# Re-pricing transfers in a kernel's own plan: side by side, with a later landing

## The chip, the core and the metric

The kernel runs on one core of one Trainium2 chip. The metric is the device time of one execution in microseconds. The core has five engines, each with an instruction queue that it works off in order: TensorE (PE: matmuls and transposes), VectorE (DVE), ScalarE (ACT), GpSimd (POOL) and SyncE (SP, which here does nothing but issue transfers). An instruction whose inputs are not there holds up everything behind it in its own queue.

## What is computed

Two layers over x of shape (32, 512, 128), that is 32 images of 512 nodes with 128 features, with one adjacency matrix of 512 x 512 shared by all. Cut to what matters:

```python
h = relu(layernorm(x))                                     # layer 0
x = x + leaky_relu(softmax_attention(h @ W, adj), 0.3)     # graph attention
h = relu(layernorm(x))                                     # layer 1
for _ in range(5):                                         # gated recurrence
    m = adj @ h                                            # for every image
    z = sigmoid(m @ w3a.T + m @ w3b.T + h @ u3.T + ...)
    r = sigmoid(m @ w4a.T + m @ w4b.T + h @ u3.T + ...)
    hv = tanh(m @ w5a.T + m @ w5b.T + (r * h) @ u5.T + ...)
    h = (1 - z) * h + z * hv
x = x + h
```

The five steps of an image depend on each other; the 32 images don't.

## The kernel before

An image goes through `layer0` once and then through `recurrence` five times. The state of an image is held turned (`hT`: features on the partitions) for the gates, and as rows (nodes on the partitions, split into a high and a low fp16 half, `hi` and `lo`) for the product with the adjacency. One step on PE is: m from `hi` and `lo` (8 matmuls, L1031), g for the reset gate (L1050, L1051), v for the candidate (L1089, L1090) and g again for the update gate (L1071). ACT takes the results out of PSUM (L1042, L1056, L1078, L1095), and DVE makes the products and the new state (L1063, L1101, L1107, L1110).

At the end of a step the new state must be turned into rows. For the first three images and near the end PE does that (`turn`, L1124). In all other steps it goes through DRAM: DVE transposes blocks of 32 x 32 (`blocks`, L1137), SP stores them (`way`, L1143), and after the store four loads fetch a quarter of the rows each (`rows`, L1148). ACT then makes `hi` (L1008) and DVE makes `lo` (L1006), and PE can start the next step. The loads wait for the store alone, and write separate partitions of the same tile.

`layer0` does the same kind of thing on POOL's queue from the fifth image on. `blockwise` turns an image in four stores and one load, once for the attention's input (`turn_a`, L733, and the load into `h0T`, L746) and once for the recurrence's (`turn_b`, and the load into `hT`). The attention's destination scores go out in four small stores (`line`, L866) and come back spread over all partitions (`es`, L879).

None of this is issued in the order of the loops. Every piece of work is a `Task` with an engine, a modelled duration, a key (its due time), the tasks that it needs and the buffers that it uses. `plan` simulates the engines: again and again it takes, among the tasks that can begin earliest, the one with the lowest key, and notes when its result is seen. The tasks are then issued in that order, and the order within each engine's queue is what the chip runs. Three things of the model concern this change:

```python
COST = {... "POOL": (650, 0, 130), "SP": (430, 0, 0)}    # ns per task: fixed, per column, until seen
seen = begin + t.ns + t.lands                            # lands: LANDING for a transfer
f.last = max(f.last, seen)                               # a buffer is free again when its last use is seen
```

A transfer takes 430 ns on SP or 650 ns on POOL to issue, and its result is seen `LANDING` ns later (1500 ns more for the big loads of `blockwise` and for `es`). A task can begin only when all that it needs is seen. Buffers are counted by tag (`BUFFERS`): there are two of `blocks` (shared by the turns of layer 0 and of the recurrence), three of `rows`, four each of `way`, `turn` and `line`, and two of `res`, the results on their way out. The plan's needs are for the order only: the waits of the program itself follow from what each instruction reads and writes.

Of the kernel before, what the change touches and what calls it, by code (L numbers as in the profile page):

```python
# [44 lines left out]
    "SP": (430, 0, 0),  # L45
}
FIRST_IDLE, IDLE = 32, 36
LANDING = 2600
BRANCH = 150

WAIT = {"DVE": 200, "ACT": 200}
# [232 lines left out]
def gat_then_gated_gnn_kernel(  # L284
# [40 lines left out]
    def add(*args, **kwargs):  # L325
        tasks.append(Task(*args, **kwargs))
        return tasks[-1]
# [127 lines left out]
    t = add("PE", [1024], soon, issue, (a_dst_loaded,), (f_as,), at=4300)  # L455
# [56 lines left out]
    t = add("POOL", [1] * 3, 0, issue, (rest_loaded,))  # L512
# [9 lines left out]
    t = add("PE", [256] * 5, 0, issue, (t,), (f_ws, f_us))  # L522
# [55 lines left out]
    t = add("DVE", [1] * 4, late, issue, (*counted, wa_made))  # L578
# [7 lines left out]
    t = add("PE", [256], late, issue, (t,), (f_viol,))  # L586
# [130 lines left out]
    def blockwise(dst, src, which, keys, needs, buffers, by_halves):  # L717


        f, way = Buffer("blocks"), Buffer("turn")  # L720

        def blocks():
            pin(nc.vector.transpose(
                new(f, f"blocks_{which}"), src().rearrange("p k d -> p (k d)")
            ))

        t = add("DVE", [512], keys(0), blocks, needs, (*buffers, f))

        def store(g):
            def issue():  # L730
                if way.tile is None:
                    new(way, f"turn_{which}", (K * P, P))
                pin(nc.gpsimd.dma_start(  # L733
                    out=way.tile.rearrange("(e r) (g q) -> g r e q", r=Q, g=G)[g],
                    in_=f.tile[ts(g, Q)].rearrange("r (e q) -> r e q", q=Q),
                ))

            return issue

        stores = []  # L740
        for g in range(G):
            stores.append(add("POOL", [1], keys(1), store(g), (t, *stores[-1:]), (f, way),
                              lands=LANDING))

        def load():
            pin(nc.gpsimd.dma_start(  # L746
                out=dst().rearrange("p (k m) -> p k m", k=K),
                in_=way.tile.rearrange("(k p) m -> p k m", k=K),
            ))

        return add("POOL", [1], keys(2), load, stores, (*buffers, way), lands=LANDING + 1500)

# [10 lines left out]
    def layer0(b):  # L763
# [7 lines left out]
        def keys(i):  # L771
            return begin + length * (base[0] + i) / parts
# [10 lines left out]
        t = relu_layernorm(h, lambda: f_x.tile, f"a{b}", keys, (loaded,), (f_x, f_h), b == 0)  # L783
        base[0] = 5
        turn = transposed if direct else blockwise
        t = turn(hT, h, f"a{b}", keys, t, (f_h, f_hT), b == 0)
# [5 lines left out]
        def hw():  # L792
            return f_hw.tile or new(f_hw, f"hw_{b}", (P, K, D + 3))
# [40 lines left out]
        if direct:  # L834
            f_es = Buffer("g", "bank")

            def spread(half):
                def issue():
                    es = f_es.tile or new(f_es, f"es_{b}")
                    for k in range(2 * half, 2 * half + 2):  # L840
                        pin(nc.tensor.transpose(
                            es[:, ts(k, P)], hw()[:, k, D + 1 : D + 2].to_broadcast([P, P]), ident
                        ))

                return issue

            t = None
            for half in range(2):
                t = add("PE", [256] * 2, keys(0), spread(half), (made[half], t), (f_hw, f_es))
        else:  # L850
            f_es, f_lines, way = Buffer("es"), Buffer("lines"), Buffer("line")
            rep = Q // K

            def gather():
                pin(nc.vector.transpose(
                    new(f_lines, f"lines_{b}", (P, Q)).rearrange("p (k e) -> p k e", k=K),
                    hw()[:, :, D + 1 : D + 2].to_broadcast([P, K, rep]),
                ))

            t = add("DVE", [64], keys(0), gather, made, (f_hw, f_lines))  # L860

            def store(k):
                def issue():
                    if way.tile is None:
                        new(way, f"line_{b}", (K, P))
                    pin(nc.gpsimd.dma_start(  # L866
                        out=way.tile[k].rearrange("(g q) -> g q", g=G),
                        in_=f_lines.tile[k * rep :: Q],
                    ))

                return issue

            stores = []
            for k in range(K):
                stores.append(add("POOL", [1], keys(1), store(k), (t, *stores[-1:]),
                                  (f_lines, way), lands=LANDING))

            def spread():
                pin(nc.gpsimd.dma_start(  # L879
                    out=new(f_es, f"es_{b}"),  # L880
                    in_=way.tile.rearrange("k p -> (k p)").partition_broadcast(P),
                ))

            t = add("POOL", [1], keys(2), spread, stores, (way, f_es), lands=LANDING + 1500)
        base[0] = 15
# [92 lines left out]
        if by_halves:  # L978
            joined = []
            for part, ks in enumerate((slice(0, K // 2), slice(K // 2, K))):  # L980
                t = add("DVE", [256], keys(0.3 * part), lambda ks=ks: leak(ks), averaged[part : part + 1],
                        (f_o,))
                joined.append(add("DVE", [256], keys(0.3 * part), lambda ks=ks: join(ks), (t,),
                                  (f_o, f_x)))
        else:
            t = add("DVE", [512], keys(0), lambda: leak(slice(0, K)), averaged, (f_o,))
# [8 lines left out]
        t = relu_layernorm(hN, lambda: x1, f"b{b}", keys, joined, (f_hN,), False)  # L995
        base[0] = 26
        halved = halves(b, hN, keys(0), t, (f_hN,))
        t = turn(lambda: hTs[b % SLOTS], hN, f"b{b}", keys, t, (f_hN,), False)
# [13 lines left out]
    def recurrence(b, step, halved, turned):  # L1012
# [5 lines left out]
        def keys(i):  # L1018
            return key + i * STEP / 4
# [19 lines left out]
        t = add("PE", [493] * K, keys(0), aggregate("hi", True), (high, *adjacency), (f_m,))  # L1039
        t = add("PE", [493] * K, keys(0), aggregate("lo", False), (t, low), (f_m,))  # L1040
# [12 lines left out]
        t = add("PE", [2048] * 2, keys(2), gate_r, (t_m, turned, *weights), (f_g, f_mT))  # L1053
# [21 lines left out]
        t = add("PE", [2048], keys(3), gate_z, (t_r,), (f_g, f_mT))  # L1075
# [16 lines left out]
        t = add("PE", [2048] * 2, keys(3), candidate, (t_rh,), (f_v, f_mT, f_rh))  # L1092
# [4 lines left out]
        t = add("ACT", [512], keys(4), tanh_v, (t,), (f_v, f_hv))  # L1097
# [14 lines left out]
        t = add("DVE", [512], keys(5), differ, (t,), (f_hv, f_d))  # L1112
        t = add("DVE", [512], keys(5), gated, (t, t_z), (f_z, f_d))
# [3 lines left out]
        if nth < 5 * SHORT or (step >= STEPS - 2 and b >= B - SHORT_END):  # L1117

            f = Buffer("o", "bank")

            def turn():
                h_ps = new(f, f"h_{b}_{step}")
                for k in range(K):
                    pin(nc.tensor.transpose(h_ps[:, ts(k, P)], hT[:, ts(k, P)], ident))  # L1124

            needs = (add("PE", [256] * K, keys(6), turn, (turned,), (f,)),)
            view = ("p k d -> p k d", {})

            def src():
                return f.tile.rearrange("p (k d) -> p k d", k=K)  # L1130
        else:


            f_b, way, f = Buffer("blocks"), Buffer("way"), Buffer("rows")

            def blocks():
                pin(nc.vector.transpose(  # L1137
                    new(f_b, f"blocks_{b}_{step}").rearrange("p (g k q) -> p g k q", g=G, k=K),
                    hT.rearrange("p (k g q) -> p g k q", g=G, k=K),
                ))  # L1140

            def store():
                pin(nc.sync.dma_start(out=new(way, f"way_{b}_{step}"), in_=f_b.tile))  # L1143

            def load(g):
                def issue():
                    rows = f.tile or new(f, f"rows_{b}_{step}", (P, G, N // G))
                    pin(nc.sync.dma_start(  # L1148
                        out=rows[ts(g, Q)],
                        in_=way.tile.rearrange("(a q) (g e) -> g q a e", a=G, g=G)[g],  # L1150
                    ))

                return issue

            t = add("DVE", [512], keys(6), blocks, (turned,), (f_b,))
            t = add("SP", [1], keys(6), store, (t,), (f_b, way), lands=LANDING)
            needs = []
            for g in range(G):
                needs.append(add("SP", [1], keys(6), load(g), (t, *needs[-1:]), (way, f),
                                 lands=LANDING))  # L1160
            view = ("p k (a q) -> p a k q", {"a": G})

            def src():
                return f.tile.rearrange("p a (k q) -> p a k q", k=K)
# [18 lines left out]
        if view[1]:  # L1183
            t = add("ACT", [480], keys(8), lower, needs, (f, f_res))
# [147 lines left out]
```

## Time and profile before

| | |
|---|---|
| runs shown | 1143.91, 1145.57, 1149.21 us; median 1145.57 |
| profiled execution | 1144.8 us; its span on the core 1142.7 us |
| granted PE clock | 1.0 |
| busy: PE, DVE, ACT, POOL | 1133.5, 940.6, 659.9, 350.0 us |
| DMA traffic | 132.88 MB, mean 116 GB/s |
| recurrence turns through DRAM | 146 stores, 584 loads |
| turns of layer 0 through DRAM | 28 images, 112 stores each of turn_a, turn_b and line |

Busy times are those of one profiled execution. PE's matmuls overlap in the record (the end of one is modelled and lies past the start of the next), so the rate at which they start says more than their busy time. The profile also gives the chain of waits that ended last, the list of who waited for whom, and for each transfer the time from its issue to its landing.

### The profile page before, as it was taken

The page shows a single profiled execution, that of the slowest core. Times are in us where ns is not written, and L with a number is a line of the kernel's source. Part 1 is how long each engine was busy: PE and PEld are TensorE (multiplying, and loading weights), DVE is VectorE, ACT ScalarE, POOL GpSimd, SP SyncE. Part 2 cuts the span into 40 slices and gives each one's busy share as a digit, 9 for nine tenths or more (in the row PEclk, how much of TensorE's full clock was granted, in tenths as well). Part 3 has the DMA queues.
Part 4 walks back from the last instruction along what each step waited for, and adds up shares of the span by engine and source line. Part 5 has one row for each costly group of instructions (what it writes and reads, how often), then busy time and mean ns, then how long its engine had stood idle before and what let it go on. Part 6 is the DMA issues. An engine that isn't in the chain of part 4 may idle for free.

```text
span 1142.7 us, 15158 instructions
## 1 busy us (share of the span) xinstructions
PE 1133.5 (99%) x4373; PEld 598.5 (52%) x4373; DVE 940.6 (82%) x2124; ACT 659.9 (58%) x1297; POOL 350.0 (31%) x503
## 2 busy tenths in 40 slices
PE   9999999999999999999999999999999999999998
PEld 8665554554555545555554555555555555444444
DVE  7888887887879979889898888799889988667664
ACT  6665656456556465647556646655655655555553
POOL 4345434123244143244413242432544331100000
PEclk9999999999999999999999999999999999999999
DMA  3114444344354444344543443452455343322311
GB/s 107 44 38 122 115 128 133 112 146 118 104 164 116 136 130 136 116 138 119 146 136 115 126 132 120 139 154 89 133 149 144 116 121 117 107 92 79 102 44 67
DMA packets 133916, 132.88 MB, mean 116 GB/s; under 512 B 22083, under 2 KB 97989, under 8 KB 133701
## 3 DMA queue, kind: packets, MB, share of 16 engines
q1 hardware_dynamic: 116066, 94.89, 26.5%
q0 software_dynamic: 17472, 36.79, 13.0%
q8 instruction: 36, 0.59, 0.2%
q14 instruction: 52, 0.42, 0.1%
q10 hardware_dynamic: 290, 0.20, 0.1%
HBM read 70.39 MB, written 61.40 MB: 115 GB/s over the span
## 4 chain that ended last, share of the span: by engine, by line
PE 91%; DVE 5%; DMA 2%; issue 1%; ACT 0%; SPq 0%; DVEq 0%; ACTq 0%
PE m L1031 23%; PE g L1071 11%; PE v L1090 11%; PE g L1050 11%; PE v L1089 11%; PE g L1051 11%; PE av L922 9%; PE hp L806 2%; DMA rows<-way 1%; DVE hT L1110 1%; DVE pt L891 1%; DVE blocks L1137 1%; DVE lo L1006 1%; PE h L1124 1%; DVE d L1101 0%
## 5 line engine op out<-in xcount | busy, mean ns | idle before, releaser
L1056 ACT ACTIVATE rs<-g,zrb 128x512 f32<-128x512 f32 x160 | 109.7, 686 | 143.9 <-PE g L1051 133.4
L1101 DVE SCALAR_TENSOR_TENSOR d<-hv,hT 128x512 f32<-128x512 f32 x159 | 108.4, 682 | 78.3 <-ACT hv L1095 78.0
L1095 ACT ACTIVATE hv<-v,vb 128x512 f32<-128x512 f32 x159 | 108.8, 684 | 104.8 <-PE v L1090 104.2
L1042 ACT COPY mT<-m 128x512 f32<-128x512 f32 x160 | 93.6, 585 | 123.7 <-PE m L1031 121.1
L1031 PE MATMUL m<-adjT,hi 128*128 128x512 f16 x640 | 162.6, 379 | 1.8 <-ACT hi L1008 1.8
L1050 PE MATMUL g<-hT,u3T 128*128 128x512 f32 x320 | 163.5, 593 | 0.0
L1051 PE MATMUL g<-mT,w4sT 128*128 128x512 f32 x320 | 163.5, 592 | 0.0
L1071 PE MATMUL g<-mT,w3dT 128*128 128x512 f32 x320 | 163.1, 593 | 0.0
L1031 PE MATMUL m<-adjT,lo 128*128 128x512 f16 x640 | 162.1, 379 | 0.4 <-DVE lo L1006 0.4
L1089 PE MATMUL v<-mT,w5sT 128*128 128x512 f32 x318 | 162.4, 592 | 0.0
L1090 PE MATMUL v<-rh,u5hT 128*128 128x512 f32 x318 | 162.4, 592 | 0.0
L1078 ACT ACTIVATE zs<-g,zrb 128x512 f32<-128x512 f32 x160 | 109.6, 686 | 59.6 <-PE g L1071 56.6
L1063 DVE SCALAR_TENSOR_TENSOR rh<-rs,hT 128x512 f32<-128x512 f32 x160 | 108.6, 682 | 40.8 <-ACT rs L1056 40.3
L922 PEld LDWEIGHTS av<-hw,pt 128*128 128x128 f32 x1024 | 122.0, 191 | 17.8 <-issue 13.6
L922 PE MATMUL av<-hw,pt 128*128 128x129 f32 x1024 | 123.2, 275 | 0.2 <-ACT adjT L497 0.2
L1110 DVE SCALAR_TENSOR_TENSOR hT<-d,hT 128x512 f32<-128x512 f32 x159 | 109.7, 690 | 11.3
L1031 PEld LDWEIGHTS <-hi 128*128 128x128 f16 x640 | 62.5, 98 | 103.0 <-issue 46.7
L1107 DVE SCALAR_TENSOR_TENSOR d<-zs,d 128x512 f32<-128x512 f32 x159 | 109.6, 689 | 4.5
L1137 DVE STREAM_TRANSPOSE blocks<-hT 128x512 f32<-128x512 f32 x146 | 102.7, 706 | 5.3 <-DMA way<-blocks 3.2
L1031 PEld LDWEIGHTS <-lo 128*128 128x128 f16 x640 | 62.4, 98 | 84.7 <-issue 14.2
L644 POOL TENSOR_TENSOR rs_b<-ve_b,mhalf 128x4 f32<-128x4 f32 x32 | 37.2, 1162 | 224.7 <-DVE ve_b L624 188.4
L1051 PEld LDWEIGHTS g<-mT,w4sT 128*128 128x128 f32 x320 | 60.7, 190 | 76.7 <-issue 71.5
(135 smaller groups left out, 1443.7 us busy)
## 6 DMA issues: line engine op xcount, KB each, us to landing
way<-blocks SPq DMA_DIRECT2D x146, 256.0 KB, 2.1
rows<-way SPq DMA_DIRECT2D x584, 64.0 KB, 2.1
x<-in_x_dram SPq DMA_DIRECT2D x32, 256.0 KB, 2.9
out_dram<-res SPq DMA_DIRECT2D x31, 256.0 KB, 2.1
turn_a<-blocks_a POOLq DMA_DIRECT2D x112, 64.0 KB, 2.3
h0T<-turn_a POOLq DMA_DIRECT2D x28, 256.0 KB, 3.5
es<-line POOLq DMA_DIRECT2D x28, 256.0 KB, 3.8
turn_b<-blocks_b POOLq DMA_DIRECT2D x112, 64.0 KB, 2.3
```

The source lines that it names most:

```text
L922: pin(nc.tensor.matmul(avs()[:, i, :], lhsT=f_pts[c].tile[:, ts(2 * part + i, P)], rhs=hw()[:, c, : D + 1], start=start, stop=(c == K - 1) ...
L1031: pin(nc.tensor.matmul(f_m.tile, lhsT=part[:, k, :], rhs=adjT[:, k, :], start=(first and k == 0), stop=(not first and k == K - 1),))
L1050: pin(nc.tensor.matmul(g, lhsT=u3T, rhs=hT, start=True, stop=False))
L1051: pin(nc.tensor.matmul(g, lhsT=w4sT, rhs=f_mT.tile, start=False, stop=True))
L1056: pin(nc.scalar.activation(new(f_r, f"rs_{b}_{step}"), f_g.tile, AF.Tanh, bias=rb, scale=0.5))
L1071: pin(nc.tensor.matmul(f_g.tile, lhsT=w3dT, rhs=f_mT.tile, start=False, stop=True, skip_group_check=True))
L1078: pin(nc.scalar.activation(new(f_z, f"zs_{b}_{step}"), f_g.tile, AF.Tanh, bias=zb, scale=0.5))
L1089: pin(nc.tensor.matmul(v, lhsT=w5sT, rhs=f_mT.tile, start=True, stop=False))
L1090: pin(nc.tensor.matmul(v, lhsT=u5hT, rhs=f_rh.tile, start=False, stop=True))
L1107: pin(nc.vector.scalar_tensor_tensor(d, f_z.tile, 1.0, d, ALU.add, ALU.mult))
L1110: pin(nc.vector.scalar_tensor_tensor(hT, f_d.tile, 0.5, hT, ALU.mult, ALU.add))
L1137: pin(nc.vector.transpose(new(f_b, f"blocks_{b}_{step}").rearrange("p (g k q) -> p g k q", g=G, k=K), hT.rearrange("p (k g q) -> p g k q", ...
```

## The change

It touches the plan's model alone, in two ways. The constant `LANDING` goes from 2600 to 5000 ns, in every place where it is used: the stores and loads of both kinds of turn, the scores' stores, and the stores of results. And the four stores of a layer-0 turn, the four stores of the scores and the four loads of a recurrence turn no longer need one another: each needs only the task before the group. The program has the same instructions on the same engines; the order in the queues is planned anew.

```diff
-LANDING = 2600
+LANDING = 5000
...
         for g in range(G):
-            stores.append(add("POOL", [1], keys(1), store(g), (t, *stores[-1:]), (f, way),
+            stores.append(add("POOL", [1], keys(1), store(g), (t,), (f, way),
                               lands=LANDING))
...
             for k in range(K):
-                stores.append(add("POOL", [1], keys(1), store(k), (t, *stores[-1:]),
+                stores.append(add("POOL", [1], keys(1), store(k), (t,),
                                   (f_lines, way), lands=LANDING))
...
             for g in range(G):
-                needs.append(add("SP", [1], keys(6), load(g), (t, *needs[-1:]), (way, f),
+                needs.append(add("SP", [1], keys(6), load(g), (t,), (way, f),
                                  lands=LANDING))
```

## The prediction

> **What bounds the kernel now.** I read the shares first, then the chain, then who TensorE (PE) waited for, then the transfers that the change re-prices. The page's first part and its chain:
>
> ```profile
> PE 1133.5 (99%) x4373; PEld 598.5 (52%) x4373; DVE 940.6 (82%) x2124; ACT 659.9 (58%) x1297; POOL 350.0 (31%) x503
> PE 91%; DVE 5%; DMA 2%; issue 1%; ACT 0%; SPq 0%; DVEq 0%; ACTq 0%
> ```
>
> PE is busy in 99% of the span and is 91% of the chain. Busy time alone can hide gaps, as matmuls overlap, so I checked the rate in the chain between 300 and 330 us:
>
> ```profile
> 299.93 3.45 PE m L1031 x16
> 303.38 0.86 PE g L1050 x2
> 304.24 0.86 PE g L1051 x2
> ...
> 327.98 1.78 PE av L922 x16
> ```
>
> A pass of m takes 3.45/16 = 0.216 us, a pass of g or v 0.43, one of av 0.111, and these rates hold all through. The stream's length follows: 1280 m x 0.2156 = 276.0, 1596 g and v x 0.429 = 684.7, 1024 av x 0.1116 = 114.2, 256 hp x 0.112 = 28.7, some 184 transposes and fillers x 0.11 = 20.2, the rest about 5: **1129 us**, the same in any order. The span is 1142.7. Of the 13.7 between, 1.4 come before PE's first matmul, 5.3 after its last, and about 7 are gaps. PE's waits, all of them:
>
> ```profile
> PE m L1031 <- ACT hi L1008: 1.8, 1, 1.8
> PE idle L434 <- POOL ident masks.py:199: 1.4, 1, 1.4
> PE m L1031 <- DVE lo L1006: 0.4, 1, 0.4
> PE h L1124 <- DVE hT L1110: 0.2, 1, 0.2
> PE av L922 <- ACT adjT L497: 0.2, 1, 0.2
> ```
>
> Only the first and third, 2.2 us, lie in the body. The first has its cause in the very transfers at issue (chain, 308 to 323 us):
>
> ```profile
> 315.59 0.43 SPq L1148
> ...
> 316.06 4.55 DMA rows<-way
> ...
> 321.13 0.61 ACT hi L1008
> ...
> 321.79 1.04 PE m L1031 x4
> ```
>
> One rows load took 4.55 us where the plan reckoned 2.6. The transfers as a whole (part 6, last column issue to landing), and the spread for the rows loads alone:
>
> ```profile
> way<-blocks SPq DMA_DIRECT2D x146, 256.0 KB, 2.1
> rows<-way SPq DMA_DIRECT2D x584, 64.0 KB, 2.1
> turn_a<-blocks_a POOLq DMA_DIRECT2D x112, 64.0 KB, 2.3
> h0T<-turn_a POOLq DMA_DIRECT2D x28, 256.0 KB, 3.5
> es<-line POOLq DMA_DIRECT2D x28, 256.0 KB, 3.8
> DMA to landing us min/median/max: 1.7/2.1/4.9
> ```
>
> So 2.6 is a fair figure for the median, 5.0 one for the worst landing.
>
> **What the skill says.** The Trainium skill, "Perfetto Trace Analysis", Identifying the Most-Contended Engine, warns that matmul busy share is a bad measure of headroom; hence the rate above. "TensorE: Matmul & The Clock Gate", Back-to-back issue gap, gives about N/2.4 + 2.5 ns for a warm isolated matmul, 216 ns at N = 512; the trace's 216 agrees, so PE has no slack inside its stream (the lower sustained figure of 131 that the section also gives is not seen here). "DMA: Bandwidth & Descriptors", Anatomy of one DMA, puts a fixed 2.0 us on a transfer, mostly the receipt of the write; the 2.1 for 64 KB and for 256 KB alike agree. Transfers side by side share that cost and transfers in a row pay it each: the change's first half matches what the hardware does, since the four loads wait only for the store.
>
> **The change part by part.** No instruction, semaphore or buffer is added or removed: 15158 instructions before and after. What changes is the order in which each engine's queue holds them.
>
> Recurrence turn (146 times; SP). Planned before: store 0.43 + 2.6, then four loads in a row, 4 x (0.43 + 2.6): 15.15 us. After: 0.43 + 5.0, four issues 4 x 0.43, 5.0: 12.15. The plan believes in rows **3.0 us sooner**. What the turn really takes: pairing the 118 turns that feed an `hi` in the trace, from the end of blocks to the last landing is 12.6 us at the median, because the plan spaced the loads 3 us apart and SP, in order, keeps them behind other images' stores; store landed to last load issued alone is 8.7. With the loads planned together, the price from the rows is 0.34 + 2.1 + 4 x 0.43 + 2.1 = 6.3 us, to which up to about 3 us of another image's store or x load standing between may come. The margin between what the plan reckons and what happens goes from some 15.15 - 12.6 = 2.6 us to 12.15 - 9 = 3 or up to 12.15 - 6.3 = 6. If all four loads landed at the worst 4.9 seen, they would still be inside the 5.0. Behind the four loads another image's store may now wait up to 4 x 0.43 = 1.7 us on SP, and its blocks buffer with it; that is inside its own margin. So I expect fewer late rows: those 1.8 us go, worth **-1 to -2 us**; what is late next is DVE's `lo` (0.4 us at 926).
>
> Stores of layer 0 (turn_a, turn_b, line; POOL). Before: 4 x (0.65 + 2.6) + 0.65 + 4.1 = 17.75; after: 4 x 0.65 + 5.0 + 0.65 + 6.5 = 14.75. Three of them per image: layer 0 is believed 9 us shorter. PE does not wait on it in the body (the waits above name no h0T or es); **0 us**, covered by the images' lead. POOL's queue: a pow (L644) can now stand behind four stores, 4 x 0.65 = 2.6 us, instead of one; rs is in layer 0 as well, where POOL idles 188 us for `ve_b` alone. Were that cover gone, one such delay per image, 28 x 2 = 56 us at most; the empty list of PE waits says it is far from that.
>
> Buffers. The plan holds a `rows` buffer (3) from its first load: shorter by 5.4 us; `way` (4) shorter by 3.0. A `blocks` buffer (2) is freed at its store's reckoned landing: a recurrence turn holds it 2.4 us longer (about 3.8 becomes 6.2), a layer-0 turn some 5.4 shorter (13.8 becomes 8.4). Per image 5 x 3.8 + 2 x 13.8 = 46.6 becomes 5 x 6.2 + 2 x 8.4 = 47.8 of 2 x 35.7 us: no scarcer. `res` likewise has two buffers for one use per image: 0. The trace does not show contention among four loads issued at once beyond their 4.9 maximum; from below it is 0, from above 2.8 us a turn (4.9 - 2.1), both inside the reckoned 5.0, so I take 0.
>
> Start and end. The first images use PE transposes, as do the last steps; the first 38 us and the tail of 5.3 after the last matmul don't change. Sum: -1 to -2, plus chance from reordering, taken as 0 to +1. Against the profiled 1144.8 (span 1142.7 and 2.1 around it), which stands 0.8 under the median 1145.57: about 1.5 off the median gives **1144.0**.
>
> **Rivals.** (1) Slower: the two `blocks` buffers. The 2.4 us longer hold makes the plan put off a third turn's DVE transpose. Among the 202 transposes of L1137 and L723 in the trace, 33 are the third within 6.2 us, short of it by 1.5 us on average; only 2 lie within 3.8. Each put-off delays one image's rows; PE shows it only where no other matmul is ready. It decides once four of these reach PE (4 x 1.5 = 6 us). If one in four does, 8 x 1.5 = 12, **1157**. For it: `blocks` waited for `way` three times already (3.2 us), and DVE is 75.8 of 80 us busy in 850 to 930, so delayed work cannot be caught up there. Against: shorter layer-0 holds, six images in flight (keys 6 apart per step, 5 per image, 5 steps), and PE's two waits in 1000 us. (2) Faster by over 0.5%: it would need 5.7 us, but gaps in the body are 2.2, and with every gap of the stream closed it would be 1142.7 - 7 + 2.9 (median less span) = **1138.6**. That asks for the cold start's gaps too, which no transfer of this kind touches. (3) The order hardly changes, as keys and not readiness decide on a full PE: **1145.6**.
>
> **How the numbers follow.** Main case (packed PE, late rows gone) 0.55, its own range 1140.5 to 1147. Order without effect, 0.17, 1143 to 1149. Slower 0.25, spread from 1151.3 to 1165. Faster 0.03. A measurement of this kernel can tell about 0.5%, 5.7 us, from no change. So same is 0.55 + 0.17 = 0.72. The range leaves out the far half of the slower case and the edge below: 1140.5 to 1156.
>
> **What would show it.** In the changed trace the four rows loads of a turn should stand together on SP (x4 in about 1.7 us), the turn's median fall from 12.6 to 7 to 9 us, PE's wait for `hi` vanish, and `ACT hi <- rows` (11.2 us in 13 waits) shrink. Turns as long as before would make rival 3 right. PE waits of 1 to 2 us each for `hi` or `lo` in the body, with `blocks` waiting for buffers more often, would make rival 1 right. The prediction is wrong if PE's waits in the body exceed some 6 us, or if PE's stream itself grows beyond 1129.

## The result and the profile after

The changed kernel takes **1142.03 us** (median of 20 runs, 1141.02 to 1145.17) against 1145.57 before (20 runs, 1143.59 to 1151.06): ratio **0.9967**, 95% interval 0.9958 to 0.9976, so 3.5 us less. Run again later beside other kernels (e4 below) it gave 0.9978, 0.9968 to 0.9988. Part of the difference between the two figures is a toss at the start: in some executions PE reaches its full rate some 5 us later, which costs about 2 us (the last section has the traces). Of the changed kernel's runs, 15 of 20 lie in its faster group (up to 1142.6 us) in the first comparison and 4 of 11 (up to 1141.6 us) in e4. The profiles of before and after both caught the early start, and their spans differ by 2.5 us. That is the better estimate of the change itself, and e4's 0.9978 agrees with it; about 1 us of the 3.5 is then the toss.

The shares and the chain of the page, for the changed kernel:

```profile
PE 1133.4 (99%) x4373; PEld 598.9 (53%) x4373; DVE 946.6 (83%) x2124; ACT 658.9 (58%) x1297; POOL 350.2 (31%) x503
PE 98%; DMA 1%; DVE 0%; ACT 0%; SPq 0%; issue 0%; DVEq 0%
```

PE's busy time is the same to 0.1 us, as the stream is. What changed is the chain: 98% of it is PE, where it was 91%. The 5% of DVE is gone, and the 2% of DMA has fallen to 1%, all of it at the start. PE's list of waits, complete:

```profile
PE idle L434 <- POOL ident masks.py:199: 1.4, 1, 1.4
PE h L1124 <- DVE hT L1110: 0.2, 1, 0.2
PE av L922 <- ACT adjT L497: 0.2, 1, 0.2
```

The two waits of the body, for `hi` (1.8) and `lo` (0.4), are gone; start and end are as they were. The work counted on each engine is the same in number too. The page's total of 15187 is 29 above the 15158 before, not equal to it as the prediction said: the difference is in semaphore waits, which follow the order. A finer measure, used below for every kernel, takes from each matmul's start to the next one's what is over its usual pace: these **body gaps**, between 40 us and the last 20, were 3.0 us before and are 0.6 after. That agrees with the profiled spans, 1142.7 and 1140.2.

The transfers themselves land as before, and what stands around them has changed. SP's queue between 311 and 323 us, first before, then after (start, duration, count of issues in a row):

```profile
310.94 2.81 SPq L1148 DMA_DIRECT2D rows<-way  x3
315.20 0.34 SPq L1143 DMA_DIRECT2D way<-blocks  x1
315.59 1.45 SPq L1148 DMA_DIRECT2D rows<-way  x3
319.15 0.34 SPq L1143 DMA_DIRECT2D way<-blocks  x1
321.25 0.78 SPq L1148 DMA_DIRECT2D rows<-way  x2
...
```

```profile
312.52 0.36 SPq L1188 DMA_DIRECT2D out_dram<-res  x1
312.97 1.83 SPq L1148 DMA_DIRECT2D rows<-way  x4
315.80 0.34 SPq L1143 DMA_DIRECT2D way<-blocks  x1
319.86 1.73 SPq L1148 DMA_DIRECT2D rows<-way  x4
```

Before, one turn's four loads were mixed with another's, with a store between them that waits for DVE. After, they stand in fours that SP issues in 1.7 to 1.8 us. A turn, from the end of blocks to the last landing, takes 7.3 us at the median of 118, where it took 12.6. (The trace gives the landing of about three loads in four; the last known one of a turn counts.) The time that rows lie ready before `hi` starts went from 2.3 to 4.7 us. Before, `ACT hi` stood among those who waited for the rows tile:

```profile
  ACT hi L1008: 11.2, 13
```

In the changed kernel it no longer does. The first line of that list there, and the landings:

```profile
  DVE lo L1006: 15.4, 18
...
DMA to landing us min/median/max: 1.7/2.1/5.1
```

The worst single landing is no earlier than before, 5.1 us against 4.9. (DVE's waits are for ACT, which makes `hi` of these rows.)

### The profile page after: what moved, and what is told of

It is laid out like the page before. It is cut to its first block, busy times and chain, and to the rows that moved or that the text cites. A ratio compares the mean times of both kernels' runs of the same rounds, so it can differ in the third digit from the quotient of the medians.

```text
span 1140.2 us, 15187 instructions
## 1 busy us (share of the span) xinstructions
PE 1133.4 (99%) x4373; PEld 598.9 (53%) x4373; DVE 946.6 (83%) x2124; ACT 658.9 (58%) x1297; POOL 350.2 (31%) x503
## 4 chain that ended last, share of the span: by engine, by line
PE 98%; DMA 1%; DVE 0%; ACT 0%; SPq 0%; issue 0%; DVEq 0%
PE m L1031 24%; PE g L1071 12%; PE g L1050 12%; PE g L1051 12%; PE v L1090 12%; PE v L1089 12%; PE av L922 10%; PE hp L806 2%; PE h L1124 1%; DMA a_sb<-in_adj_dram 0%; PE idle L434 0%; DMA cols<-in_L_gnn_w_b_dram 0%; PE t_b L701 0%; PE t_a L701 0%; PE es L841 0%; PE end L1241 0%
## 5 line engine op out<-in xcount | busy, mean ns | idle before, releaser
L733 POOL DMA_DIRECT2D turn_b<-blocks_b x112 | 73.6, 663 | 91.1 <-DVE blocks_b L723 89.4
```

## The experiments

The first theory was the prediction's: rows came late, now they come early, and that is all. Its rival: the gain lies in layer 0, whose three turns are believed shorter. After the first four runs neither stood alone. The theory that replaced them has **two causes**: rows must really arrive before the plan reckons them, and the plan must have images ready at all times. One table first; then the runs. "Believed" is the plan's time for a recurrence turn from its store, "real" the trace's median from the end of blocks to the last landing, "spare" the median time that rows lie ready before `hi`, "late" how often `hi` waited for rows. "Planned idle" is read from the plan and not from the chip: `plan` of each kernel can be run by itself, and this is the time for which its simulation leaves PE without work, from 40 us on and up to 20 before its end. Real, spare, late and body gaps are of one profiled execution each.

| kernel | believed | real | spare | late | planned idle | body gaps | ratio to before (95%) |
|---|---|---|---|---|---|---|---|
| before | 15.15 | 12.6 | 2.3 | 13 | 3.8 | 3.0 | 1 |
| after | 12.15 | 7.3 | 4.7 | 0 | 0.4 | 0.6 | 0.9967 (0.9958 to 0.9976) |
| e4 after, again | 12.15 | 7.4 | 4.7 | 0 | 0.4 | 0.6 | 0.9978 (0.9968 to 0.9988) |
| e1 recurrence only | 12.15 | 7.1 | 5.0 | 1 | 4.3 | 2.2 | 0.9990 (0.9983 to 0.9997) |
| e2 layer 0 only | 15.15 | 12.4 | 2.7 | 18 | 0.6 | 3.7 | 1.0011 (1.0002 to 1.0020) |
| e3 side by side, 2600 | 7.35 | 6.2 | 0.7 | 29 | 0.6 | 6.9 | 1.0052 (1.0032 to 1.0072) |
| e5 chained, 1990 | 12.10 | 10.3 | 1.8 | 32 | 0.1 | 10.6 | 1.0090 (1.0074 to 1.0106) |
| e12 side by side, 3800 | 9.75 | 6.6 | 2.9 | 3 | 0.9 | 3.2 | 0.9999 (0.9990 to 1.0008) |
| e7 side by side, 5600 | 13.35 | 7.7 | 5.5 | 0 | 0.0 | 0.2 | 0.9977 (0.9968 to 0.9987) |
| e6 side by side, 6500 | 15.15 | 8.0 | 6.7 | 0 | 4.5 | 2.7 | 0.9987 (0.9975 to 0.9999) |
| e8 side by side, 8000 | 18.15 | 9.1 | 8.2 | 1 | 95.3 | 67.5 | 1.0574 (1.0556 to 1.0592) |
| e9 8000, three blocks | 18.15 | 10.5 | 7.4 | 0 | 6.0 | 1.5 | 0.9983 (0.9972 to 0.9993) |
| e10 8000, store at 2600 | 12.75 | 6.6 | 6.0 | 0 | 6.1 | 3.7 | 0.9998 (0.9989 to 1.0007) |
| e11 e1 with LEAD 13 | 12.15 | 6.8 | 5.4 | 0 | 0.3 | 0.2 | 0.9971 (0.9960 to 0.9981) |

**e1 and e2: each half alone.** e1, against the kernel before:

```diff
-            t = add("SP", [1], keys(6), store, (t,), (f_b, way), lands=LANDING)
+            t = add("SP", [1], keys(6), store, (t,), (f_b, way), lands=5000)
...
-                needs.append(add("SP", [1], keys(6), load(g), (t, *needs[-1:]), (way, f),
-                                 lands=LANDING))
+                needs.append(add("SP", [1], keys(6), load(g), (t,), (way, f),
+                                 lands=5000))
```

e2 is the change with these two places, and the results' stores, as before (2600, loads chained).

> Only the recurrence's turn is re-priced (its store and its four loads at 5000, loads side by side); layer 0's stores and the results stay as before. Late-rows theory (the stated one): the gain came from rows arriving well inside what the plan reckons, so all of it is here: ratio to before about 0.997, no PE wait for hi or lo in the body, turn 7 to 9 us. Rival, layer-0 theory: the gain came from layer 0's three turns being believed 3 us shorter each, so that images are ready earlier and PE always has something in hand: then nothing here, ratio 1.000, and PE gaps of 2 us or more remain in the body.

> Only layer 0's turns are re-priced (stores side by side, landings 5000 and 6500); the recurrence's turn and the results stay at 2600 with chained loads. Late-rows theory: rows still take about 12.6 us against 15.15 reckoned, so a late landing still reaches PE: ratio 0.999 to 1.000. Layer-0 theory: the whole gain, ratio 0.997, and the body's gaps gone although the rows are as tight as before.

e1 brought a third to a half of the gain, e2 a small loss, where both theories had expected no loss. The late rows went in e1 but for one of 0.2 us, as the first theory said, but a wait of another kind took their place. The one new line among PE's waits in e1:

```profile
PE g L1071 <- ACT rs L1056: 1.2, 1, 1.2
```

and its chain before that wait, from 832 us on:

```profile
832.73 0.86 DVE st_a L615 x4
833.60 0.61 DVE blocks_a L723
834.21 0.06 DVE nb_b L672
...
834.28 0.88 ACT hN L681 x2
835.16 0.57 ACT hv L1095
835.74 0.77 ACT hN L681 x2
836.51 0.58 ACT rs L1056
...
837.14 1.12 PE g L1071 x2
```

PE had nothing left but the next gate of an image that it had just served, and that gate's `rs` stood on ACT behind four `hN` of layer 0: a new image arriving just when it is needed. No transfer is in this chain. A single wait could be chance, but this one was planned: e1's plan, run by itself, leaves PE idle for 0.93 us before this very gate, and the PE task after it is the first product of a new image. Over the body it plans 4.3 us of idle time, as the kernel before does (3.8). e2 plans only 0.6, so it is layer 0's half that fills the plan; but e2 has 18 late rows, which is the kernel before's trouble.

**e3, e5: the belief without the truth.** e3 takes the kernel before and drops the two `*stores[-1:]` and the `*needs[-1:]` only; e5 keeps them and sets LANDING to 1990, so that a turn is believed as short as in the changed kernel while its loads stay spread out.

> The groups are side by side but LANDING stays 2600: the plan believes in rows after 3.03 + 1.72 + 2.6 = 7.35 us, where the chip needs 6.3 at best and 7.3 at the median of the changed kernel. Late-rows theory: the margin is gone, some half of the rows come late, each late one by 1 to 3 us: gaps of 5 to 30 us on PE, ratio 1.005 to 1.025. Layer-0 or belief-only theory: as the changed kernel or slightly better, 0.997, since the plan believes in even shorter turns.

> The groups stay chained and LANDING is 1990, so that a recurrence turn is believed to take 5 x (0.43 + 1.99) = 12.1 us, as in the changed kernel (12.15), but its loads are planned 2.4 us apart. Two-cause theory, formed after the first four runs: the time needs both a plan that has images ready at all times and rows that really arrive before they are reckoned. Here the first holds and the second does not (loads spread as before, about 10 to 10.5 us real against 12.1): rows late in 15 or more of the turns, ratio 1.000 to 1.003. Belief-only theory: the same belief gives the same time, 0.997 to 0.998.

> The changed kernel once more, as the measure for the three beside it on the same chip: ratio 0.9967 within 0.9958 to 0.9976, and no PE wait for hi or lo in the body.

e4 repeats the changed kernel; its 0.9978 lies just outside the range that was expected of it. e3 is at the lower edge of what the late-rows theory gave, 1.0052. `hi` waited 29 times, 32.5 us, and PE for a layer-0 turn besides:

```profile
PE g L1071 <- ACT rs L1056: 1.8, 3, 0.9
PE g L1050 <- DMA hT<-turn_b: 1.4, 3, 0.8
```

e5 refutes the belief-only theory: the same belief as the changed kernel, 12.1 us, and as good a plan (0.1 us of idle time) gave 1.0090 against 0.9978. It was worse than I expected, probably because LANDING 1990 is also below the median landing of 2.1, for layer 0's stores too.

**e12, e7, e6: how late to reckon.** The changed kernel with LANDING 3800, 5600 and 6500.

> Side by side with LANDING 3800: believed turn 4.23 + 1.72 + 3.8 = 9.75 us, between e3 (7.35, ratio 1.005) and the changed kernel (12.15, 0.997 to 0.998). Two-cause theory: a turn takes about 6.7 us here, margin 3 us, a handful of rows late and rarely onto PE: ratio 0.997 to 0.999. If 5.0 for the single worst landing were needed: 1.000 to 1.003.

> Side by side with LANDING 5600: believed turn 6.03 + 1.72 + 5.6 = 13.35 us, a little more margin than the changed kernel. Two-cause theory: both conditions hold, ratio 0.996 to 0.998, body gaps under 1 us; it can hardly beat the changed kernel, whose body gaps are 0.6 us already. Rival (buffers of blocks held longer): 6.8 us holds begin to put off turns, ratio 0.999 or above.

> Side by side with LANDING 6500: the believed recurrence turn is 6.93 + 1.72 + 6.5 = 15.15 us, just that of the kernel before, but the loads stand together. Two-cause theory: no late rows, but the plan is short of ready images in places as before and PE then waits inside a step (for rs or mT): ratio 0.998 to 1.000. Margin-only theory (late rows alone): margin is larger still, 0.997 or below.

5600 is as good as 5000. 6500, with the believed turns just those of the kernel before (15.15 us in the recurrence and, by the prediction's sum, 17.75 in layer 0) and rows never late, keeps about half: the margin-only theory falls. Its plan has 4.5 us of idle time, and the body gaps of 2.7 us are a wait for `hi` of 0.6 and one for `rs` of 0.3 in PE's list, the rest shorter pieces. 3800 missed its 0.997 to 0.999. Rows are hardly late (3 times); its chain shows another place where a landing counts:

```profile
223.48 0.70 DVE blocks L1137
224.18 0.03 DVE nb_a L672
224.21 3.49 DMA way<-blocks
...
227.79 0.71 DVE blocks L1137
228.50 0.58 DVE rh L1063
...
229.13 1.12 PE v L1090 x2
```

DVE stood in front of a transpose that needed the other blocks buffer until a slow store had landed, 3.49 us, and `rh`, for which PE waited 0.8 us, stood behind it. In all, `blocks` waited 7.2 us in 7 times there, 2.5 in 4 in the changed kernel.

**e8, e9, e10: the two blocks buffers.** LANDING 8000; then with `"blocks": 3` for `"blocks": 2`; then with two again, and the recurrence's store alone reckoned at 2600.

> Side by side with LANDING 8000: believed turn 8.43 + 1.72 + 8.0 = 18.15 us, against some 8 to 11 real. Two-cause theory: rows never late, but the plan runs short of ready images all through, and the order it writes down then makes PE wait inside steps where it could have had other work: slower, ratio 1.01 to 1.05. Rival (a pessimistic plan costs nothing on the chip, as queues run ahead of it): 0.997 to 1.000.

> As e8 (side by side, LANDING 8000) with three buffers of blocks instead of two, on the chip and in the plan. Buffer theory (rival 1 of the prediction, at a hold of 8 us and more): what made e8 slow by 5.7% was the plan putting off DVE's transposes until a blocks buffer is reckoned free, so nearly all comes back: ratio 0.998 to 1.002. Latency theory: the believed turn of 18.15 us itself starves PE, whatever the buffers: 1.04 or more.

> As e8, but the recurrence's store alone is reckoned at 2600 (its loads stay at 8000), so that the plan frees a blocks buffer as early as in the kernel before; the chip has two buffers as ever. If it is the plan's belief in the hold and not the real buffers that cost e8 its time: ratio 0.997 to 1.002. If the chip really lacks a third buffer: 1.02 or more, with DVE waiting for the stores.

e8 is 5.7% slower, more than the 1.01 to 1.05 expected, with a single late row (0.9 us):

```profile
PE m L1031 <- ACT hi L1008: 25.4, 24, 1.8
PE g L1071 <- ACT rs L1056: 12.2, 15, 1.7
PE m L1031 <- DVE lo L1006: 6.6, 10, 1.9
```

`hi` is late here, but not for want of rows: they lie ready 8.2 us before it at the median, and at least 4.6 us in the 15 of the 24 waits that stand on a turn through DRAM (the other 9 are for a new image). ACT had no idle time before any of these 15; `hi` stood late in its queue, where the plan had put it. SP waited 409.5 us for DVE's transposes (384.4 in the changed kernel), yet no transpose waited for a store to land: for the blocks tile, e8's trace names nothing that its engine sat idle for. The chip had a buffer free; the plan, which holds one for 8 us and more after each store, had put the transposes later in DVE's queue (2.9 us after they could begin, at the plan's median, against 0.3 in the changed kernel). The plan itself has 95.3 us of idle time on PE here. With a third buffer nearly all of it comes back (0.9983), and so it does when the plan merely releases the same two buffers earlier (0.9998). e9 shows that the hold was what cost, as its turn is still believed to take 18.15 us. e10, which has two real buffers, shows that it was the believed hold, though its believed turn is shorter as well (12.75).

**e11: layer 0 earlier by another way.** e1 with LEAD 13 for 11.

> As e1 (only the recurrence's turn re-priced) and LEAD 13 instead of 11: layer 0 is keyed two steps of 6.1 us earlier, while its turns are still reckoned at 17.75 us. Two-cause theory: what layer 0's re-pricing gave was images ready sooner, which an earlier key gives as well: e1's wait inside a step (1.2 us for rs) goes, body gaps under 1 us, ratio 0.997 to 0.998 as the changed kernel. Rival (layer 0's stores must stand together on POOL): as e1, 0.999.

0.9971, and body gaps of 0.2 us. Layer 0's turns are priced as before and their stores chained, so their standing together on POOL is not needed. That images are ready earlier is. e7 and e11 are the best of the others, and neither beats the changed kernel beyond the intervals.

**The two causes side by side.** The kernels that plan under 0.5 us of idle time and have no late row (the changed one, e7, e11) keep body gaps of 0.2 to 0.6 us. Those with a plan nearly as full but late rows (e2, e3, e5, and e12 with 3) have 3.2 to 10.6. Those with at most one late row but 4.3 to 6.1 us of planned idle time (e1, e6, e9, e10) have 1.5 to 3.7. e8 is this trouble at its worst, and the kernel before has both. The planned idle time isn't met to the microsecond on the chip (e9: 6.0 planned, 1.5 measured), but it tells which order is short of work.

## Why the prediction was right, and where not

**The bound, right.** PE's work was the same (4373 matmuls, 1133.4 us busy), and 1139.8, the span of e11, is the lowest profiled. "Faster by over 0.5%" was out of reach, as rival 2 said. That a measurement tells only 0.5% from no change was too cautious: 20 runs on each side told 0.33%, with an interval of 0.1% to either side.

**Late rows, right in mechanism.** The step from 12.6 to "7 to 9" for a turn was met (7.3), the spare time grew from 2.3 to 4.7 against the step's "3 or up to 6", and the wait of 1.8 us for `hi` went, with the one of 0.4 for `lo`. The price of -1 to -2 was that of this part alone: e1 measured 0.9990, -1.1 us.

**Layer 0 at 0 us: the term that failed.** I took the empty list of PE waits on `h0T` and `es` as proof that layer 0's pace costs nothing. It costs in the plan, where PE is left without a task (3.8 us before, 0.6 with this half alone), and on the chip where PE waits inside a step for want of another image, and such a wait is booked to `rs` or `hi`. e1, without this half, keeps body gaps of 2.2 us; e11, with layer 0 merely keyed earlier, has 0.2 and the whole gain. From 0.9990 to 0.9978 or 0.9967 the term is an estimated 1.4 to 2.6 us (the results' stores, which e1 leaves at 2600, are in it), and with e1's 1.1 it makes -2.5 to -3.7. Nor do the parts add up as the prediction's sum has it: alone, in e2, this half costs 1.3 us, because rows are late there. The measured -3.5 lies inside the range, and outside the -1.5 that I summed up; the sum as written, -1 to -2 with chance of 0 to +1, even centres on -1. So the size came out near by a wide range, and not because this part was foreseen. "Chance from reordering, 0 to +1" hid the same thing: e1's `rs` wait is no chance but planned, and the changed kernel has none.

**Rival 1, the blocks buffers, right in mechanism and wrong in place.** At 5000 it did nothing: the waits of `blocks` for `way` fell from 3.2 us to 2.5 (with layer 0's transposes, which use the same two buffers, 5.2 both times), as the per-image sum of holds (46.6 to 47.8 of 71.4 us) suggested. My count of 33 transposes within 6.2 us overstated it; that a turn put off by 1.5 us still has its rows in time, with 4.7 us to spare, is the likely reason. It decides between 6500 (0.9987) and 8000 (1.0574), steeply. The prediction's own sum says so: with holds of 9.2 and 11.4 us an image needs an estimated 68.8 of the 71.4 us at 8000, and 58.3 at 6500. e9 and e10 show that it is this and not the believed latency.

**Rival 3 did not happen:** the order changed on all engines, and the time with it.

What stays open: LEAD 13 was not tried on the kernel before, so what an earlier layer 0 gives without the recurrence's half is known from e2 alone. Which instruction's place in the new order is due to which of the two re-pricings was not traced one by one; the halves were only tried whole.

## What to carry to other kernels

When an order is made by a model with due times, a price in the model does two things: it decides when results are believed, and where the transfers stand in their queue. Compare the believed time with the real one of the whole turn, queue included, and with the landing's tail rather than its median; then ask what the price does to buffers that the model holds for the same time. Such a plan can also be run without the chip: its own idle time on the busiest engine showed here which re-pricing fills the order, before any trace. What it can't show is whether the transfers keep its times; that is what the trace is for. On an engine without slack, a wait for the next gate inside a step can mean that no other work was ready, whatever releaser the list names: look for who should have had work there.

## What the runs showed of the hardware

**The landing's tail.** In the profiles of these kernels, loads of 64 KB land in 2.0 to 2.2 us at the median and in up to 4.3 to 6.1, whether issued 3 us apart or together: side by side they are no slower (medians of 2.1 before and after). The Trainium skill's "DMA: Bandwidth & Descriptors", Anatomy of one DMA, gives a fixed cost of about 2.0 us plus the bytes over 436 GB/s for transfers that GpSimd issues. For the 64 KB stores of layer 0 that makes an estimate of 2.15 us; in the kernels before and after they took 2.2 to 2.4 at the median, and up to 5.5. The traces agree near the median and not in the tail, and the plan has to price the tail. SP's loads are not what that section describes.

**The start's toss.** PE's first matmuls run at half rate. In the changed kernel's two profiles the pair at 5.39 us, the same instructions, took (first profile, then e4):

```profile
5.39 0.69 PE L450 MATMUL as_ps<-avecs,ones 1*128 1x256 f32 x2
```

```profile
5.39 1.22 PE L450 MATMUL as_ps<-avecs,ones 1*128 1x256 f32 x2
```

The traces' record of the granted clock has full rate from 5.3 us on in the first and from 10.4 in e4, 5.1 us later. The spans differ by 2.0 us, 1140.2 and 1142.2, with the same body gaps. e4's runs lie in two groups accordingly, 1141.0 to 1141.6 and 1142.9 to 1143.9. The profiles of e3, e5, e7 and e10 have the late start too (9.8 to 10.8 us), all others the early one (4.2 to 6.2). "TensorE: Matmul & The Clock Gate", Part 1, describes a free-running activity window of about 3.4 us after which the clock opens. The traces agree on the window's length: the full clock lasted 1133.2 us in the first profile and 1129.8 in e4, 3.4 less. Why the start moved by 5.1 and not by 3.4 us is not shown. For differences of 0.3% the toss is a thing to know: compare many runs, or the body gaps.
